# A two-layer hybrid kernel: result places taken in the tile's own unit, moments and first loads issued earlier, three Newton steps, first keys on VectorE

## The chip, the cores and the metric

The kernel runs on one core of one Trainium2 chip. The metric is the device time of one execution in microseconds; the number for a kernel is the median of its timed runs. For the kernel before, three runs gave 991.65, 992.59 and 993.67 us. One further execution was recorded by the hardware profiler.

A core has five engines that work side by side, each on its own instructions in their order: PE (TensorE: matrix products and transposes; its weight loads are listed apart, as PEld), DVE (VectorE), ACT (ScalarE), POOL (GpSimd) and SP (SyncE, which here issues DMA transfers). PE writes to PSUM, from where DVE and ACT take the results into SBUF. An engine waits where an operand is missing or a buffer is still being read.

## The reference

Everything is float32. `x` has the shape [16, 256, 128]: 4096 tokens of 128 channels. Four blocks follow one another, each added to its input:

```python
x = x + attn_a(layernorm(x))     # 16 heads of 8, within blocks of 64 tokens of a sequence
x = x + ffn(layernorm(x))        # router over 8 experts, the best 2 per token
x = x + attn_b(layernorm(x))     # over the first axis (16), for each of 256 positions
x = x + ffn(layernorm(x))        # the same experts and weights again

# ffn
logits = flat_x @ Wr
top_vals, top_idx = top_k(logits, 2);  rw = softmax(top_vals)
g, u = flat_x @ Wg[e], flat_x @ Wu[e]            # [128 -> 512] for an expert e
h = silu(g) * u
out = sum over the two e of rw[e] * (h @ Wd[e]) / sqrt(12)
```

The attention A part has query, key and value biases; attention B first multiplies by `w_tor`, has a toroidal bias on its scores and an output projection. Layer norms have no scale or shift: `(x - mean) / sqrt(var + 1e-5)`.

## The kernel before

**Tokens.** The stream x stays in SBUF as four quarters `xq[q]`, each of 8 groups of 128 rows. A half of a quarter is four groups, 512 rows.

**Stages.** The outer loop runs over two layers, and in each over eight halves `hq` (quarter and half). Layer 0 runs `attention_a` of a half (24 steps), layer 1 `attention_b` (20 steps). After the second half of a quarter comes its `router`: layer norm F, logits, best two, ranks within each expert and, from the second quarter on, the tables of tiles. GpSimd puts each token's normalised row twice into `sorted_in` in DRAM, sorted by expert, with an indirect DMA (L787: one for 128 rows). `experts(layer)` takes the sorted rows as tiles: 256 rows in the first two lists, 128 rows in the last list, whose tiles are known only after the last router. `fetch` (L955, L972) loads a tile's rows `xin` and the three weight matrices `w` of its expert (768 KB) on SP's queue. `turned` makes the tile's transposed rows (`xt` on PE L993, `xT` by ACT L995). Then come the products `g` and `u` (L1055), tanh on ACT (`th` L1066), `th` and `h` on DVE (L1067, L1069), the products down into `acc` (L1006), scaling to `yo` on ACT (L1017), and indirect DMAs by GpSimd to `results` (L1021). The place of each result row stands as one more column of `xin`; the DVE operation `to` (L990) takes it and combines it with the place for padded rows.

The rows of `results` come back with `back` loads (L1102, on SP) and are added to `xq` on DVE (L1117). For layer 1, `begin_b(q)` does this for a quarter, normalises it (`normal_b`) and prepares queries and keys. The numbering `back_0_7` means layer 0, seventh half.

**Order.** `weave(main, *sides)` advances a main generator and hands out the steps of side generators evenly between two of its steps: a side is `(generator, steps, first, last)`. In attention A the sides are the router of the quarter before, `prepare_a` of the next half (layer norm, keys, queries), the `moments` of the half after next, and units of the experts. A scheduler then sets each engine's order from the instructions' priorities and its own cost model, so an engine's order is not exactly that of the program. Each engine executes that fixed order.

**Moments and deviation.** `moments` makes mean and variance on DVE (`st`, `mv`, `ve`); the reciprocal deviation `rs` is a power on GpSimd (L324), or, for attention B (`here=True`), Newton's iteration on DVE (L296-303), where each instruction needs the one before. `layernorm_t` then forms `shift` on DVE (L338), normalises on ACT (`ln`, L345) and transposes on PE (`lnp`, L357).

**Scores of attention A.** Keys and queries are made from PSUM by `four` on ACT (L391), four instructions of 512 columns each. Score products are `sc_A` (L496, PE), the row maximum `mx_A` (L504, DVE), the difference `ex_A` (L505, DVE, which frees the score's PSUM buffer), the exponential (L509, ACT).

In `turned`, called for the next tile while a tile is in work, the first statements are:

```python
to = p12.tile([P, TT // P], I32, tag="to", name=f"to_{s}_{i}")
nc.vector.tensor_tensor(to[:, 0:n], t[:, 0:n, C + 1], elsewhere, ALU.max)
pt = psum(f"xt_{s}_{i}")
```

and in the loop over `hq`:

```python
if hq + 2 < 2 * NQ:
    sides.append((moments_a(hq // 2 + 1, half), 2, n // 2, n))
```

Of the kernel before, what the change touches and what calls it, by code (L numbers as in the profile page):

```python
# [11 lines left out]
I32 = mybir.dt.int32  # L12
# [7 lines left out]
P = 128  # L20
# [94 lines left out]
def hybrid_kernel(  # L115
# [22 lines left out]
    p1 = ctx.enter_context(tc.tile_pool(name="p1", bufs=1))  # L138
    p2 = ctx.enter_context(tc.tile_pool(name="p2", bufs=2))
    p4 = ctx.enter_context(tc.tile_pool(name="p4", bufs=4))  # L140
    p12 = ctx.enter_context(tc.tile_pool(name="p12", bufs=12))
    p3 = ctx.enter_context(tc.tile_pool(name="p3", bufs=3))
    p_in = ctx.enter_context(tc.tile_pool(name="p_in", bufs=2 + AHEAD))
    dram = ctx.enter_context(tc.tile_pool(name="dram", bufs=1, space=bass.MemoryType.DRAM))
# [149 lines left out]
    def rsqrt(out, v, name):  # L294
        seed = p1.tile([P, NG], I32, tag="seed", name=f"seed_{name}")
        work = p1.tile([P, NG], F32, tag="newton", name=f"newton_{name}")  # L296
        nc.vector.tensor_scalar(seed, v.bitcast(I32), 1, None, ALU.logical_shift_right)
        nc.vector.tensor_scalar(seed, seed, -1, 0x5F3759DF, ALU.mult, ALU.add)
        y = seed.bitcast(F32)
        for _ in range(4):  # L300
            nc.vector.scalar_tensor_tensor(work, y, -0.5, y, ALU.mult, ALU.mult)
            nc.vector.tensor_tensor(work, work, v, ALU.mult)
            nc.vector.scalar_tensor_tensor(out, work, 1.5, y, ALU.add, ALU.mult)
            y = out
# [24 lines left out]
    def layernorm_t(q, halves, name, put, keep=None):  # L329
        mv, rstd = stat.pop(name)  # L330
        shift = p2.tile([P, NG], F32, tag="shift", name=f"shift_{name}")
        ln = {}
        for half in halves:
            some = slice(4 * half, 4 * half + 4)
            if keep is None:
                ln[half] = p2.tile([P, 4, C], F32, tag="ln", name=f"ln_{name}_{half}")
            behind_now(
                nc.vector.scalar_tensor_tensor(  # L338
                    shift[:, some], mv[:, some, 0], -1.0, rstd[:, some], ALU.mult, ALU.mult
                )  # L340
            )
            for i in range(4):
                g = 4 * half + i
                behind_act(
                    nc.scalar.activation(  # L345
                        ln[half][:, i, :] if keep is None else keep(g), xq[q][:, g, :],
                        AF.Identity, bias=shift[:, g : g + 1], scale=rstd[:, g : g + 1],
                    )
                )
                if i == 1:  # L350
                    yield
            yield
        for half in halves:
            pt = psum(f"lnp_{name}_{half}")
            for i in range(4):
                g = 4 * half + i
                nc.tensor.transpose(  # L357
                    pt[:, i * P : (i + 1) * P],
                    ln[half][:, i, :] if keep is None else keep(g), ident,
                )  # L360
            put(half, pt)
            yield
# [25 lines left out]
    def four(put, product, scales, biases):  # L388
        for j in range(4):
            behind_act(  # L390
                nc.scalar.activation(  # L391
                    *put(j, product), AF.Identity, bias=biases[:, j : j + 1],
                    scale=scales[:, j : j + 1],
                )
            )
            if j % 2:
                yield

    def product(src, w, name):
        p = ps_gu.tile([P, CH], F32, tag="gu", name=name)  # L400
# [64 lines left out]
    def moments_a(q, half):  # L465
        return moments(q, [half], f"A{q}_{half}", "A")

    def prepare_a(q, half):
        n = f"A{q}_{half}"
        lnT = p2.tile([P, CH // BS, 2, BS], F32, tag="src", name=f"lnT_{n}")  # L470
        qT = p2.tile([P, CH // BS, 4, BS], F32, tag="qT", name=f"q_{n}")
        kx = p2.tile([P, 4, CH], F32, tag="kx", name=f"k_{n}")

        def put(_, pt):
            nc.scalar.copy(*spread(lnT, pt, 2))

        yield from layernorm_t(q, [half], n, put)
        yield from keys(kx, lnT[:, :, 0], wk_sb, B_K, n)
        ready[q, half] = lnT, qT, kx
        yield from queries(qT, lnT[:, :, 0], wq_sb, B_Q, n)  # L480

    def attention_a(q, half):
# [57 lines left out]
    def normal_b(q):  # L540
        lnT = p1.tile([P, BS, S], F32, tag="lnT", name=f"lnB_{q}")

        def put(half, pt):
            nc.scalar.copy(  # L544
                lnT.rearrange("c t s -> c s t")[:, 8 * half : 8 * half + 8, :],
                pt.rearrange("c (s t) -> c s t", t=BS),
            )

        yield from moments(q, range(2), f"B{q}", "B", here=True)
        yield from layernorm_t(q, range(2), f"B{q}", put)  # L550
        ready[q] = lnT.rearrange("c t s -> c (t s)")

# [392 lines left out]
    def experts(layer):  # L945
# [37 lines left out]
                follow(product.ins, stepped)  # L983
            stepped[0] = product.ins

        def turned(li, i, t, elsewhere):
            s = f"{layer}_{li}"
            n = SIZES[li] // P
            to = p12.tile([P, TT // P], I32, tag="to", name=f"to_{s}_{i}")
            nc.vector.tensor_tensor(to[:, 0:n], t[:, 0:n, C + 1], elsewhere, ALU.max)  # L990
            pt = psum(f"xt_{s}_{i}")
            for b in range(n):
                nc.tensor.transpose(pt[:, b * P : (b + 1) * P], t[:, b, 0:C], ident)  # L993
            xT = p2.tile([P, TT], F32, tag="xT", name=f"xT_{s}_{i}")
            nc.scalar.copy(xT[:, 0 : n * P], pt[:, 0 : n * P])  # L995
            return xT, to

# [37 lines left out]
        for at, (li, i) in enumerate(todo):  # L1037
# [3 lines left out]
            if at == 0:  # L1041
                fetched += [fetch(*todo[0]), fetch(*todo[1])]
                begun = 2
                xT, to = turned(*todo[0], fetched[0][0], fetched[0][2])
            t, w, _ = fetched.pop(0)
            acc = ps_acc.tile([P, 512], F32, tag="acc", name=f"acc_{s}_{i}")
            for part in range(NHC // n):
                m = f"{s}_{i}_{part}"
                hcs = range(n * part, n * part + n)

                def product(k, name):
                    p = ps_gu.tile([P, CH], F32, tag="gu", name=f"{name}_{m}")
                    for j, hc in enumerate(hcs):
                        step(
                            nc.tensor.matmul(  # L1055
                                p[:, j * size : (j + 1) * size],
                                lhsT=w[:, k, hc * P : (hc + 1) * P], rhs=xT[:, 0:size],
                                start=True, stop=True,
                            )
                        )  # L1060
                    return p

                pg = product(0, "g")
                pu = product(1, "u")
                th = p2.tile([P, CH], F32, tag="th", name=f"th_{m}")
                turn_of[0] = nc.scalar.activation(th, pg, AF.Tanh, scale=0.5).ins  # L1066
                nc.vector.scalar_tensor_tensor(th, th, 1.0, pg, ALU.add, ALU.mult)  # L1067
                h = p2.tile([P, CH], F32, tag="h", name=f"h_{m}")
                beat[0] = nc.vector.tensor_tensor(h, th, pu, ALU.mult).ins  # L1069

                wanted = at + 2 if size == TT else min(begun + 1, at + AHEAD)
                while begun < len(todo) and part == 0 and begun <= wanted:
                    fetched.append(fetch(*todo[begun]))
                    begun += 1
                if part == 0 and at + 1 < len(todo):
                    following = turned(*todo[at + 1], fetched[0][0], fetched[0][2])
                if pending is not None:
                    down(*pending)
                pending = (li, i, t, w, to, acc, hcs, h)
                yield  # L1080
            xT, to = following
        down(*pending)
        yield

# [98 lines left out]
        yield from normal_b(q)  # L1183
        yield from prepare_b(q, 0)

    BEGIN_A, BEGIN_B = 3 + 4, 5 + 10 + 5
    ALONE = 8

    FIRST = BEGIN[0] + ALONE
# [5 lines left out]
    for layer in range(2):  # L1195
# [10 lines left out]
        for hq in range(2 * NQ):  # L1206
# [5 lines left out]
            if layer == 0:  # L1212
# [4 lines left out]
                    first = n // 6 if hq == 0 else 0  # L1217
                    sides.append((prepare_a((hq + 1) // 2, 1 - half), BEGIN_A, first, 2 * n // 3))
                if hq + 2 < 2 * NQ:
                    sides.append((moments_a(hq // 2 + 1, half), 2, n // 2, n))  # L1220
                wanted, goal = 0, OWN.get(hq, 0)
            else:
                main = attention_b(q, half)
# [2 lines left out]
                elif q < NQ - 2:  # L1226
                    sides.append((begin_b(q + 1), BEGIN_B, 0, 4 * n // 5))
                wanted, goal = (0, GOAL[hq]) if q < NQ - 1 else (1, OWN[hq])
            goal = max(goal, unit[wanted])
            sides.append((units(wanted, goal), goal - unit[wanted], 0, n))  # L1230
            weave(main, *sides)
            if half == 0:
                continue
            run(routing)
            if layer == 1:
                finish_b(q)
                if q == NQ - 2:
                    weave(begin_b(q + 1), (units(1, ALONE), ALONE, 0, BEGIN_B))
            routing = router(layer, q)
        weave(routing, (units(layer, EARLY), EARLY - unit[layer], 0, ROUTER))  # L1240
        run(units(layer, BEGIN[0]))
# [46 lines left out]
```

## Time and profile before

| | |
|---|---|
| median of the timed runs | 992.59 us (991.65 to 993.67) |
| the profiled execution | 941.87 us |
| its span on the core | 939.9 us |
| its mean granted TensorE clock | 0.941 of full speed |
| PE waits at 357.0 and 802.1 us, `u` behind DVE `th` | 5.62 and 5.17 us |
| PE wait at 490.1 us, `lnp_B` behind ACT `ln_B` | 6.61 us |
| PE wait at 643.5 us, `xt` behind the load of `xin` | 6.58 us |
| DVE `th` L1067 (128x512), 142 times | mean 683 ns |
| DVE `va` L443 (128x256 from PSUM) | 0.42 us |
| ACT `xT` L995 (128x256 from PSUM) | 0.37 us |
| ACT keys and queries L391 (128x512 from PSUM) | 0.79 us |

The profiled execution was shorter than the timed ones by 50.7 us. The page does not tell why; all times inside the profile add up to the profiled execution's.

A row of groups or of the timeline names the engine, the line and the operation as output <- inputs. In square brackets, or after the second bar, stands how long the engine had been idle before and which operation's end released it. "Busy in slices" is the busy share in tenths, of 40 equal parts of the span; PEclk is the TensorE clock granted in each, 9 for 90% or more. Records of the granted clock further give stretches at half clock to a microsecond.

### The profile page before, as it was taken

How to read it: one execution, taken by the hardware profiler on the slowest of the kernel's cores; microseconds unless marked ns; L12 is line 12 of the kernel's file. 1: busy time of each engine (PE TensorE's matmuls, PEld its weight loads, DVE VectorE, ACT ScalarE, POOL GpSimd, SP SyncE). 2: the span in 40 equal slices, each digit the busy share in tenths (PEclk: the TensorE clock that was granted, in tenths of full speed). 3: DMA queues.
4: the chain of work that ended last, by engine and by line, in shares of the span. 5: the costliest groups of instructions: out<-in, count | busy, mean ns of one | idle time of the engine just before them, and what ended most of it. 6: DMA issues, size and time to landing. Idle time of an engine off the chain costs nothing.

```text
span 939.9 us, 20600 instructions
## 1 busy us (share of the span) xinstructions
PE 822.3 (87%) x7582; PEld 709.2 (75%) x7582; DVE 552.7 (59%) x1653; ACT 449.2 (48%) x921; POOL 341.6 (36%) x381
## 2 busy tenths in 40 slices
PE   4999799888999997997976979995889999799983
PEld 2777587767889886997764757894668888799983
DVE  2556554564766773456592673683567687355563
ACT  4667367266445332443645635732664533244431
POOL 2113262262256474332101162262314747433321
PEclk9999988799999998999996987998989999899997
DMA  7800010016223626998410023216410452799993
GB/s 165 259 26 1 13 35 2 15 33 237 90 81 109 222 91 217 329 330 322 164 47 1 5 76 88 81 42 227 170 44 27 144 202 89 245 332 331 341 394 109
DMA packets 67011, 134.80 MB, mean 143 GB/s; under 512 B 9088, under 2 KB 46720, under 8 KB 66912
## 3 DMA queue, kind: packets, MB, share of 16 engines
q1 hardware_dynamic: 56400, 114.70, 36.5%
q0 software_dynamic: 8640, 17.97, 5.5%
q8 instruction: 60, 0.98, 0.4%
q10 hardware_dynamic: 1872, 0.83, 0.4%
q14 instruction: 39, 0.32, 0.1%
HBM read 112.33 MB, written 27.43 MB: 149 GB/s over the span
## 4 chain that ended last, share of the span: by engine, by line
PE 41%; DVE 8%; ACT 5%; DMA 4%; issue 2%; POOL 1%; SPq 0%; DVEq 0%; POOLq 0%; ACTq 0%
PE u L1055 9%; PE acc L1006 9%; PE g L1055 9%; PE v_B L437 3%; PE sc_B L600 3%; PE o_B L637 2%; DMA xin<-sorted_in 1%; PE t_B L624 1%; DMA w<-w_all 1%; PE xt_B L559 1%; ACT ln_B L345 1%; DVE th L1067 1%; PE k_B L401 1%; PE xt L993 1%; ACT lnB L544 1%
## 5 line engine op out<-in xcount | busy, mean ns | idle before, releaser
L1021 POOL DMA_INDIRECT results<-yo,to x142 | 137.3, 967 | 248.0 <-ACT yo L1017 178.4
L1067 DVE SCALAR_TENSOR_TENSOR th<-th,g 128x512 f32<-128x512 f32 x142 | 97.0, 683 | 135.4 <-ACT th L1066 134.8
L1055 PE MATMUL u<-xT,w 128*128 128x128 f32 (+1 forms) x864 | 156.7, 316 | 16.3 <-DVE th L1067 16.3
L1055 PE MATMUL g<-xT,w 128*128 128x128 f32 (+1 forms) x864 | 156.5, 316 | 6.4 <-DMA w<-w_all 3.9
L1006 PE MATMUL acc<-w,h 128*128 128x128 f32 x1136 | 155.6, 279 | 1.4 <-DVE h L1069 0.9
L787 POOL DMA_INDIRECT sorted_in<-rows,pos_i_F x128 | 132.1, 1032 | 64.3 <-issue 37.3
L1006 PEld LDWEIGHTS acc<-w,h 128*128 128x128 f32 x1136 | 144.5, 195 | 5.8 <-ACT yo L1017 1.6
L1055 PEld LDWEIGHTS u<-xT,w 128*128 128x128 f32 x864 | 126.5, 196 | 25.8 <-DVE th L1067 18.2
L1066 ACT ACTIVATE th<-g 128x512 f32<-128x512 f32 x142 | 85.0, 598 | 114.9 <-PE g L1055 111.6
L1055 PEld LDWEIGHTS g<-xT,w 128*128 128x128 f32 x864 | 121.8, 195 | 15.8 <-ACT xT L995 6.7
L1069 DVE TENSOR_TENSOR h<-th,u 128x512 f32<-128x512 f32 x142 | 97.1, 683 | 8.8 <-PE u L1055 0.7
L496 PE MATMUL sc_A<-k_A,q_A 128*128 128x256 f32 x256 | 80.6, 434 | 17.9 <-DVE ex_A L505 13.3
L1017 ACT ACTIVATE yo<-acc,xin 128x128 f32<-128x128 f32 x142 | 48.6, 366 | 65.3 <-PE acc L1006 62.8
L526 PEld LDWEIGHTS o_A<-va,eT_A 128*64 128x64 f32 x1024 | 62.2, 142 | 16.6 <-issue 6.9
L995 ACT COPY xT<-xt 128x128 f32<-128x128 f32 (+1 forms) x108 | 32.2, 298 | 80.6 <-PE xt L993 74.5
L496 PEld LDWEIGHTS sc_A<-k_A,q_A 128*128 128x128 f32 x256 | 47.3, 211 | 28.8 <-issue 8.9
L526 PE MATMUL o_A<-va,eT_A 128*64 128x18 f32 x1024 | 67.0, 216 | 0.8 <-ACT eT_A L519 0.7
L504 DVE TENSOR_REDUCE mx_A<-sc_A 128x8 f32<-128x512 f32 x64 | 43.5, 679 | 30.3 <-PE sc_A L496 30.2
L519 ACT COPY eT_A<-t_A 128x512 f32<-128x512 f32 x64 | 36.2, 587 | 44.7 <-PE t_A L515 44.3
L536 POOL TENSOR_TENSOR xq<-xq,att_A 128x128 f32<-128x128 f32 x32 | 14.6, 456 | 116.1 <-DVE att_A L456 89.6
L509 ACT ACTIVATE ex_A<-ex_A 128x512 f32<-128x512 f32 x64 | 39.9, 635 | 31.0 <-DVE ex_A L505 30.8
L505 DVE TENSOR_TENSOR ex_A<-sc_A,mx_A 128x512 f32<-128x512 f32 x64 | 42.8, 680 | 2.0 <-PE t_A L515 1.1
(178 smaller groups left out, 1236.9 us busy)
## 6 DMA issues: line engine op xcount, KB each, us to landing
w<-w_all SPq DMA_DIRECT2D x108, 768.0 KB
back<-results SPq DMA_DIRECT2D x14, 512.0 KB, 4.8
xin<-sorted_in SPq DMA_DIRECT2D x74, 66.0 KB, 3.9
xin<-sorted_in SPq DMA_DIRECT2D x34, 132.0 KB, 3.0
results<-yo,to POOLq DMA_INDIRECT x142, 3.8
w_all<-in_wg SPq DMA_DIRECT2D x1, 2048.0 KB, 15.3
w_all<-in_wu SPq DMA_DIRECT2D x1, 2048.0 KB
w_all<-in_wd SPq DMA_DIRECT2D x4, 512.0 KB
```

Source lines behind the costliest of these rows:

```text
L496: nc.tensor.matmul(sc[:, v * 4 * BS : (v + 1) * 4 * BS], lhsT=qT[:, blk, 2 * v : 2 * v + 2, :].rearrange("p r k -> p (r k)"), rhs=kx[:, :, ...
L504: nc.vector.tensor_reduce(mx[:, 0:8], sc3, AX.X, ALU.max)
L505: beat[0] = nc.vector.tensor_tensor(ex[:, b], sc3, mx[:, 0:8].unsqueeze(2).to_broadcast([P, 8, BS]), ALU.subtract,).ins
L526: nc.tensor.matmul(po[b * BS : (b + 1) * BS, i * 18 : (i + 1) * 18], lhsT=eT[:, b, 2 * v + i % 2, u * BS : (u + 1) * BS], rhs=vt[:, b, 2 * ...
L787: put_row = nc.gpsimd.indirect_dma_start(out=sorted_in[layer], out_offset=bass.IndirectOffsetOnAxis(ap=pos_i[:, k, g : g + 1], axis=0), in ...
L1006: nc.tensor.matmul(acc[:, b * C : (b + 1) * C], lhsT=h[:, j * size + b * P : j * size + (b + 1) * P], rhs=w[:, 2, hc * C : (hc + 1) * C], ...
L1017: nc.scalar.activation(y[:, b, :], acc[:, b * C : (b + 1) * C], AF.Identity, scale=t[:, b, C : C + 1],)
L1021: put_row = nc.gpsimd.indirect_dma_start(out=results[layer], out_offset=bass.IndirectOffsetOnAxis(ap=to[:, b : b + 1], axis=0), in_=y[:, b ...
L1055: nc.tensor.matmul(p[:, j * size : (j + 1) * size], lhsT=w[:, k, hc * P : (hc + 1) * P], rhs=xT[:, 0:size], start=True, stop=True,)
L1066: turn_of[0] = nc.scalar.activation(th, pg, AF.Tanh, scale=0.5).ins
L1067: nc.vector.scalar_tensor_tensor(th, th, 1.0, pg, ALU.add, ALU.mult)
L1069: beat[0] = nc.vector.tensor_tensor(h, th, pu, ALU.mult).ins
```

## The change

Six edits:

- `to` leaves `turned` and becomes `places`, called in the tile's own unit, after `h` of its first part. The pool of 12 buffers goes; `to` now has 4. Instructions are the same.
- Newton's iteration has three steps instead of four.
- `layernorm_t` yields once more between the ACT normalisations and the transposes where it treats two halves (attention B), and `normal_b` once between moments and normalisation. `BEGIN_B`, the number of steps of `begin_b`, goes from 20 to 22.
- Moments for attention A are spread from a quarter to the middle of the main loop instead of from its middle to its end.
- The experts' generator yields after its first two fetches. In layer 0 it is started ahead of the seventh half (`hq == 6`), whose units then begin after a sixth of the loop; in layer 1 ahead of `finish_b` of the third quarter, and the units beside the last `begin_b` begin after a quarter of it.
- The first half's keys and queries come from `keys_and_queries`: both products first, then in two halves of 256 columns the keys on VectorE and the queries on ScalarE.

```diff
-        for _ in range(4):
+        for _ in range(3):
             nc.vector.scalar_tensor_tensor(work, y, -0.5, y, ALU.mult, ALU.mult)
...
+        if len(halves) > 1 and keep is None:
+            yield
         for half in halves:
             pt = psum(f"lnp_{name}_{half}")
...
+    def keys_and_queries(kx, qT, src):
+        pk, pq = product(src, wk_sb, "k_first"), product(src, wq_sb, "q_first")
+        for half in range(2):
+            cols = slice(half * CH // 2, (half + 1) * CH // 2)
+            some = slice(4 * half, 4 * half + 4)
+            for j in range(4):
+                nc.vector.tensor_scalar(
+                    kx[:, j, cols], pk[:, cols], k_sb[:, K_HM + j : K_HM + j + 1],
+                    k_bias[B_K][:, j : j + 1], ALU.mult, ALU.add,
+                )
+                nc.scalar.activation(
+                    qT[:, some, j, :], pq[:, cols].rearrange("p (a k) -> p a k", k=BS),
+                    AF.Identity, bias=q_bias[B_Q][:, j : j + 1], scale=q_scale[:, j : j + 1],
+                )
...
         yield from layernorm_t(q, [half], n, put)
+        ready[q, half] = lnT, qT, kx
+        if (q, half) == (0, 0):
+            keys_and_queries(kx, qT, lnT[:, :, 0])
+            return
...
         yield from moments(q, range(2), f"B{q}", "B", here=True)
+        yield
...
-        def turned(li, i, t, elsewhere):
+        def turned(li, i, t):
             s = f"{layer}_{li}"
             n = SIZES[li] // P
-            to = p12.tile([P, TT // P], I32, tag="to", name=f"to_{s}_{i}")
-            nc.vector.tensor_tensor(to[:, 0:n], t[:, 0:n, C + 1], elsewhere, ALU.max)
             pt = psum(f"xt_{s}_{i}")
...
+        def places(li, i, t, elsewhere):
+            n = SIZES[li] // P
+            to = p4.tile([P, TT // P], I32, tag="to", name=f"to_{layer}_{li}_{i}")
+            nc.vector.tensor_tensor(to[:, 0:n], t[:, 0:n, C + 1], elsewhere, ALU.max)
+            return to
...
                 fetched += [fetch(*todo[0]), fetch(*todo[1])]
                 begun = 2
-                xT, to = turned(*todo[0], fetched[0][0], fetched[0][2])
-            t, w, _ = fetched.pop(0)
+                yield
+                xT = turned(*todo[0], fetched[0][0])
+            t, w, elsewhere = fetched.pop(0)
...
                 beat[0] = nc.vector.tensor_tensor(h, th, pu, ALU.mult).ins
+                if part == 0:
+                    to = places(li, i, t, elsewhere)
...
-    BEGIN_A, BEGIN_B = 3 + 4, 5 + 10 + 5
+    BEGIN_A, BEGIN_B = 3 + 4, 5 + 12 + 5
...
-                    sides.append((moments_a(hq // 2 + 1, half), 2, n // 2, n))
+                    sides.append((moments_a(hq // 2 + 1, half), 2, n // 4, n // 2))
...
+            first = 0
+            if layer == 0 and hq == min(OWN):
+                next(tiles[0])
+                first = n // 6
             goal = max(goal, unit[wanted])
-            sides.append((units(wanted, goal), goal - unit[wanted], 0, n))
+            sides.append((units(wanted, goal), goal - unit[wanted], first, n))
...
             if layer == 1:
+                if q == NQ - 2:
+                    next(tiles[1])
                 finish_b(q)
                 if q == NQ - 2:
-                    weave(begin_b(q + 1), (units(1, ALONE), ALONE, 0, BEGIN_B))
+                    weave(begin_b(q + 1), (units(1, ALONE), ALONE, BEGIN_B // 4, BEGIN_B))
```

## The prediction

> **What bounds the kernel now.** I read the page's first two blocks first, for the engine that sets the end.
>
> ```profile
> PE 822.3 (87%) x7582; PEld 709.2 (75%) x7582; DVE 552.7 (59%) x1653; ACT 449.2 (48%) x921; POOL 341.6 (36%) x381
> PE   4999799888999997997976979995889999799983
> PEclk9999988799999998999996987998989999899997
> ```
>
> TensorE is busy 87% of 939.9 us and no other engine passes 59%; the chain that ended last is PE for 41% too. So only three things shorten the span: less PE work (the change has none: the matmuls are the same), shorter PE gaps, and fewer spells of half clock, the 8s and 7s of PEclk. Going through PE and weight loads together I find 87 us of idle in some forty gaps, and in the clock records fifteen half-clock spells of 3.4 to 13.7 us, together 112 us. An operation is worth what it takes from one of these gaps or spells, and nothing elsewhere. The waits, ordered by engine and releaser (sum, count, longest), say which gaps the change can reach:
>
> ```profile
> DVE to L990 <- DMA xin<-sorted_in: 35.3, 16, 7.9
> PE sc_A L496 <- DVE ex_A L505: 13.3, 11, 4.0
> DVE shift_A L338 <- POOL rs_A L324: 12.1, 6, 4.9
> PE lnp_A L357 <- ACT ln_A L345: 8.9, 1, 8.9
> ```
>
> **1. Moments of attention A sooner** (quarter instead of half of the main loop, to be ended at its middle). The timeline at 112-118 us shows what late moments cost (start, busy, engine, operation, idle before and its releaser):
>
> ```profile
> 114.69 0.96 POOL L787 DMA_INDIRECT sorted_in<-rows,pos_i_F  x1 [0.30 <-issue]
> 115.67 1.04 POOL L324 TENSOR_TENSOR rs_A<-ve_A,minus_half 128x4 f32<-128x4 f32 x1
> 116.75 0.16 DVE L338 SCALAR_TENSOR_TENSOR shift_A<-mv_A,rs_A 128x4 f32<-128x4 f32 x1 [4.93 <-POOL rs_A L324]
> ...
> 117.58 2.08 PE L496 MATMUL sc_A<-k_A,q_A 128*128 128x256 f32 x4 [3.13 <-DVE ex_A L505]
> ```
>
> POOL works in order: rs_A, the power that makes the next quarter's reciprocal deviation, stands behind four puts of sorted rows, 1.27 us apart. VectorE waits 4.93 us for it at shift_A; ex_A, behind shift_A, frees the score buffer, so PE stops 3.13 us. In the new order rs_A stands ahead of the copy of the rows and of all puts of that router: this wait goes. Nothing replaces it: ex_A's operands are ready, and the puts, 1.0 us later, have no reader for some 90 us. The same at 187.4: shift_A waits 3.41 us, PE 1.95 us at lnp_A. After both stand half-clock spells: 116.1 for 6.8 us, 191.2 for 3.4 us. In these the PE does half its work, so they cost 3.4 and 1.7 us.
>
> ```profile
> 110.00:120.00 10.00, 6.65 (x55) 5.43 (x56) 4.10 (x15) 3.86 (x8) 7.83 (x9) 0.81 0.13 43
> 180.00:190.00 10.00, 8.02 (x61) 6.67 (x60) 5.14 (x22) 3.45 (x7) 8.10 (x9) 0.78 0.10 34
> ```
>
> (Columns: window, its length, busy PE, PE loads, DVE, ACT, POOL, then the granted clock: 0.81 and 0.78.)
>
> Here a rule speaks against my sum. The Trainium skill, "TensorE: Matmul & The Clock Gate", section "HAM oscillation", has the clock fall on PE idle of more than about 3.4 us. Neither gap, 3.13 and 1.95 us, is that long, so by the rule the spells come from something else and stay: gain 3.1+1.9 = 5.1 us. By the rows, spells follow stretches whose busy share is only 51-57% (112.7-119) or 52% (187.8-191): gain 5.1+3.4+1.7 = 10.2 us. The rows are this kernel's, so I take 10.2. The rule has this much for it: windows 69-73% busy near 100 us had no spell, so gap and spell aren't one to one.
>
> Of 209.7-213.8 (4.0 us idle, then a 3.4-us spell) I take half: 2.0 + 0.8. There VectorE has the router's moments and tables too, and the new order sets the first expert tile's products behind the score products sc_A of the third and fourth group of the last half, where it was the third alone. About 9.7 us of VectorE work stands before the fourth against 7.7 us of PE work, so 2 us of idle stay. Two jams of VectorE at 101-105 and 171-175 (1.6 and 2.3 us of PE idle), where moments of the next quarter lie now beside max and exponent of scores: 0.9 each. Against these: moments moved to the first half of the loop lie where the normalisation ahead of the router (F) lies. A half's statistics are 0.9 us of VectorE work and three pairs of halves move: 0 to +3, I take +1.8, as PE is 80-99% busy there with products already issued. The spells at 157.1 (13.7) and 177.6 (6.8), after windows 66-79% busy, may go or stay, 0 to -10.2; their own gaps aren't touched, I take 0. Sum: -10.2 - 2.8 - 1.8 + 1.8 = **-13.0** (-24 to -6).
>
> **2. Places of results in the tile's own unit.** The row promises most: 35.3 us of VectorE waits in 16 places. But the largest are these, at the tile lists' ends:
>
> ```profile
> 801.90 0.96 POOL L787 DMA_INDIRECT sorted_in<-rows,pos_i_F  x1 [0.30 <-issue]
> ...
> 804.47 0.33 SPq L955 DMA_DIRECT2D xin<-sorted_in  x1
> ...
> 806.44 0.16 DVE L990 TENSOR_TENSOR to<-xin,behind 128x1 int32<-128x1 f32 x1 [7.45 <-DMA xin<-sorted_in]
> 807.25 2.08 PE L1055 MATMUL u<-xT,w 128*128 128x256 f32 x4 [5.17 <-DVE th L1067]
> ```
>
> The last put leaves POOL at 801.9, xin starts at 804.5, `to` at 806.4, and th, behind it on VectorE, lets PE go after 5.2 us. The twin lies at 357.0-362.7 (5.6 us, `to` waits 7.90). In the order of the changed program `to` of the first two tiles of the last list stands where it stood, ahead of the th of the tile before, in both layers: a scheduler sets the instructions, and the moved line did not move these. So 7.90+1.62+7.45+1.62 = 18.6 of the 35.3 us stay, with both gaps and their two 6.8-us spells. The other 16.7 us lie beside a PE with queued work (of the gaps over 1 us only 760.8, 1.17, and small ones at 313-316, 0.9, meet them). `to` later delays no put: results wait for yo, a full tile later. **-2** (-3 to 0; if the two had moved too, -10 to -17 more).
>
> **3. First keys on VectorE.** At the start ScalarE makes four keys (13.77-16.55) and then four queries; the first score product waits until 17.94, the first max until 20.91. The new keys: 8 of 128x256 from PSUM, near the va row of that shape, 0.42 us, so 3.4 us in two halves of 1.7; queries 8 of half width, near the xT copy, 0.37, or half the spacing of 512-wide ones, 0.35, plus start-up, say 0.45. Query product done at 15.4, half the queries by 17.3, where the fourth was done at 19.2: score products of the first half end 1.8 us sooner. **-1.8** (-2.5 to 0). Nothing else is on VectorE there but the moments of the other half (they'd cost 0.9).
>
> **4. Newton, steps and loads of layer 1.** Three dependent instructions of 0.2 us go from each of four deviations of attention B: 0.6 us each, and in each the PE waits at lnp_B (2.28 at 442, 6.61 at 490, 3.48 at 557), so they count: B0 -0.6, B1 -1.3 (one add of 0.64 us moves behind it as well), B2 -0.8. The extra steps put work between normalisation and transposes, which PE can run instead of waiting. At the beginning of the last part, PE waits 6.58 us for xin and 1.2 for w: issuing the fetches ahead of back_0_7 (two queued loads of 512 KB ahead of them on SP today) brings w 0.8-1.5 us sooner. back_0_7 then lands near 654.6 behind 1.8 MB of tiles; its adds stand behind h at about 657, so I see no stall. -1.5. **Sum -4.2** (-8 to +2).
>
> **Total.** -13.0 - 2.0 - 1.8 - 4.2 = **-21.0 us**, from 941.87 in the profiled execution to 920.9. The median of the timed runs is 992.59, 50.7 us more, which the page doesn't explain; I carry the microseconds over: 992.6 - 21.0 = **971.6**.
>
> **Rivals.**
> - *Large gain:* spells go with the jams, at 157, 177 and in part at 443-505 too: -10.2 more in A, about -5 in B: 992.6 - 36.2 = **956**. For it: 20 us of spells follow windows 66-79% busy. Against: their gaps have releasers the change leaves alone (ln_F, k_A).
> - *Little left:* PE takes up the gained microseconds in the next wait: the router's tables on VectorE (taken, rank) and POOL's puts still end when they did, and both list-end gaps are set by puts. Then only start and Newton stay, -4: **988**. For: POOL 36% busy but back to back from 324 to 362. Against: those puts are tied to PE's tiles, and move up with them.
> - *Slower,* one mechanism: in the last half of attention A the first expert products stand behind the fourth score product. If VectorE, with four groups of F moments ahead of it, comes 3 us later than I say, the gap of 4.0 becomes 7 or more, and the clock falls for 13.7 us, as after 6.61 at 490; with xin of the first tiles displaced and back_0_7 late by 4 us in B, +3 +6.8 +4 and A's gain only -8: +6, **998**. It decides from a gap above 7 us at 210-217. Against: VectorE has 3.1 us of idle at 205-216.
> - That the change doesn't do what it says is, for the two large waits of part 2, my forecast already.
>
> **Numbers.** My forecast 0.55, large gain 0.15, little left 0.14, slower 0.16. The range: own range of the forecast 962-983; reaching to the rivals, **956 to 993**, which leaves out most of "slower" and the low half of "large gain". A difference below 0.2% (2 us) can't be told from none. Faster: 0.55+0.15+0.11 = 0.81; same 0.05; slower 0.14.
>
> **What would show it.** rs_A no longer releases shift_A with over 1 us; no PE gap of 3 us at 114 and no half clock within 110-120 and 188-195; `to` waits for xin only at the lists' ends, about 18 us; gaps of about 5 us at 357 and 802, moved up by what is saved; first max at about 19.1 us; PE idle near 70 us in place of 87. Wrong if clock spells come at new places in attention A, if PE waits at 205-217 for more than 4 us, or if back_0_7 becomes a releaser of PE.

## The result and the profile after

| | median | ratio to before (95% interval) |
|---|---|---|
| before, beside it | 992.88 us (991.65 to 993.67) | |
| changed kernel | 1007.71 us (1003.94 to 1009.86) | 1.0141 (1.0095 to 1.0188) |

The change makes the kernel slower by 14.8 us, where 21 us less were forecast. The changed kernel's page, for the lines shown of before (the last two rows are from the chain that ended last, by engine and by line):

```profile
PE 838.3 (84%) x7582; PEld 714.5 (71%) x7582; DVE 555.7 (55%) x1649; ACT 447.5 (45%) x921; POOL 342.2 (34%) x381
...
PE   5999798889988879979869678967787888799983
...
PEclk9999799999999989998979779987998999999997
...
PE 44%; DVE 16%; DMA 13%; issue 11%; ACT 8%; POOL 4%; another core or an unknown queue 3%; SPq 0%; POOLq 0%; DVEq 0%; ACTq 0%
DMA results<-yo,to 10%; PE acc L1032 6%; PE g L1082 6%; PE u L1082 6%; PE o_A L546 6%; PE sc_A L516 5%; POOL results L1047 3%; PE t_A L535 2%; PE o_B L658 2%; PE sc_B L621 2%; DVE th L1094 2%; PE v_B L454 2%; PE v_A L446 1%; DVE ex_A L525 1%
```

A second trace of the kernel before, of the same kind of chip as this one (before_again, in the experiments below), has TensorE busy for 85% of its span, and its chain by engine is this:

```profile
PE 62%; DVE 12%; ACT 8%; issue 6%; another core or an unknown queue 4%; POOL 4%; DMA 3%; SPq 0%; POOLq 0%; DVEq 0%; ACTq 0%
```

So TensorE does the same 7582 products in about the same share of the span. What is new is the chain that ended last: it rests on transfers for 13% in place of 3%, and 10% is `results<-yo,to`. The waits of the changed kernel (total, times, longest) say who waits for it:

```profile
DVE to L1021 <- DMA results<-yo,to: 130.9, 67, 6.4
...
PE u L1082 <- DVE th L1094: 18.8, 16, 3.0
...
DVE to L1021 <- DMA xin<-sorted_in: 13.4, 4, 6.9
...
DVE shift_A L337 <- POOL rs_A L323: 1.2, 1, 1.2
```

In the kernel before, first profile, the first of these rows was this:

```profile
DVE to L990 <- DMA results<-yo,to: 1.6, 1, 1.6
```

(In before_again it is 1.3 us.) So the wait that the moments were to remove is gone (12.1 us to 1.2), and a new one has come: VectorE waits 130.9 us, 67 times, for result rows to land before it may take the next place.

One thing has to be known for the rest: the kernel before took a different time in different sets of runs, a median of 992.9, 996.5 and 998.6 us in three and 937.0 us in the fourth. The last three were taken on three chips; I call the two kinds slow and quick chips. The first profile, 941.9 us, looks like one of a quick chip. Ratios are therefore always to the kernel before on the same chip, and traces are compared only where they are of the same kind.

### The profile page after: what moved, and what is told of

Same layout as the page of the kernel before. It is cut to its first block, busy times and chain, and to the rows that moved or that the text cites. A ratio compares the mean times of both kernels' runs of the same rounds, so it can differ in the third digit from the quotient of the medians.

```text
span 1002.2 us, 20600 instructions
## 1 busy us (share of the span) xinstructions
PE 838.3 (84%) x7582; PEld 714.5 (71%) x7582; DVE 555.7 (55%) x1649; ACT 447.5 (45%) x921; POOL 342.2 (34%) x381
## 4 chain that ended last, share of the span: by engine, by line
PE 44%; DVE 16%; DMA 13%; issue 11%; ACT 8%; POOL 4%; another core or an unknown queue 3%; SPq 0%; POOLq 0%; DVEq 0%; ACTq 0%
DMA results<-yo,to 10%; PE acc L1032 6%; PE g L1082 6%; PE u L1082 6%; PE o_A L546 6%; PE sc_A L516 5%; POOL results L1047 3%; PE t_A L535 2%; PE o_B L658 2%; PE sc_B L621 2%; DVE th L1094 2%; PE v_B L454 2%; PE v_A L446 1%; DVE ex_A L525 1%
## 5 line engine op out<-in xcount | busy, mean ns | idle before, releaser
L1047 POOL DMA_INDIRECT results<-yo,to x142 | 142.6, 1004 | 267.1 <-ACT yo L1043 201.4
L1082 PE MATMUL u<-xT,w 128*128 128x128 f32 (+1 forms) x864 | 160.0, 319 | 21.2 <-DVE th L1094 18.8
L1032 PE MATMUL acc<-w,h 128*128 128x128 f32 x1136 | 159.8, 283 | 11.5 <-issue 3.7
L1082 PE MATMUL g<-xT,w 128*128 128x128 f32 (+1 forms) x864 | 159.1, 320 | 7.6 <-DMA w<-w_all 5.1
L808 POOL DMA_INDIRECT sorted_in<-rows,pos_i_F x128 | 127.3, 995 | 101.3 <-issue 43.9
L1032 PEld LDWEIGHTS acc<-w,h 128*128 128x128 f32 x1136 | 147.0, 198 | 19.3 <-issue 9.0
L1082 PEld LDWEIGHTS u<-xT,w 128*128 128x128 f32 x864 | 126.7, 197 | 35.6 <-DVE th L1094 24.1
L1082 PEld LDWEIGHTS g<-xT,w 128*128 128x128 f32 x864 | 124.2, 198 | 17.4 <-issue 8.3
L516 PE MATMUL sc_A<-k_A,q_A 128*128 128x256 f32 x256 | 73.9, 407 | 10.5 <-DVE ex_A L525 6.0
L1021 DVE TENSOR_TENSOR to<-xin,behind 128x1 int32<-128x1 f32 x74 | 11.8, 160 | 107.0 <-DMA results<-yo,to 94.6
L516 PEld LDWEIGHTS sc_A<-k_A,q_A 128*128 128x128 f32 x256 | 45.2, 201 | 20.6 <-issue 6.1
```

The lines of the kernel that those rows point to most:

```text
L516: nc.tensor.matmul(sc[:, v * 4 * BS : (v + 1) * 4 * BS], lhsT=qT[:, blk, 2 * v : 2 * v + 2, :].rearrange("p r k -> p (r k)"), rhs=kx[:, :, ...
L808: put_row = nc.gpsimd.indirect_dma_start(out=sorted_in[layer], out_offset=bass.IndirectOffsetOnAxis(ap=pos_i[:, k, g : g + 1], axis=0), in ...
L1032: nc.tensor.matmul(acc[:, b * C : (b + 1) * C], lhsT=h[:, j * size + b * P : j * size + (b + 1) * P], rhs=w[:, 2, hc * C : (hc + 1) * C], ...
L1047: put_row = nc.gpsimd.indirect_dma_start(out=results[layer], out_offset=bass.IndirectOffsetOnAxis(ap=to[:, b : b + 1], axis=0), in_=y[:, b ...
L1082: nc.tensor.matmul(p[:, j * size : (j + 1) * size], lhsT=w[:, k, hc * P : (hc + 1) * P], rhs=xT[:, 0:size], start=True, stop=True,)
```

## The experiments

**Theory W**, formed from the new row: `to` has 4 buffers now in place of 12. A buffer is free only when the put that reads it has landed, so `to` of a tile waits for the puts of the tile four before, and everything behind `to` on VectorE (th, h, vb) waits too. **Theory S**: the extra steps and earlier starts disorder attention B. **Theory U**: moving `to` costs by itself, through the order that the scheduler makes.

The first set, all on one chip, has the kernel before unchanged and three mixtures.

> The kernel before, unchanged, to see its profile beside its timed runs (the first profile, 941.9 us, was 51 us under the median). If that profile was an execution of another kind, this one lies near 992, its added time spread over the attention B and expert stages, with the same half-clock pattern as the changed kernel's; ratio 1.000 within 0.002. If the profiled execution is always shorter than the timed ones, the profile lies near 942 again.

> The changed kernel, with the tile pool of the places `to` back at 12 buffers in place of 4. Theory W (with 4 buffers each place waits on VectorE until the result puts of the tile four before have landed, and th and h stand behind it): the loss goes and the other parts' gain of some 8 us shows: 975 to 990 us, ratio to before 0.985 to 0.997. Theory S (the steps and earlier starts put the attention B stage out of order): stays at 1003 to 1010. Theory U (the move of the place itself, whatever the buffers): also stays above 1000.

```diff
+    p12 = ctx.enter_context(tc.tile_pool(name="p12", bufs=12))
...
-            to = p4.tile([P, TT // P], I32, tag="to", name=f"to_{layer}_{li}_{i}")
+            to = p12.tile([P, TT // P], I32, tag="to", name=f"to_{layer}_{li}_{i}")
```

> The kernel before with edit 1 alone: places taken in the tile's own unit, 4 buffers. Theory W: slower than before by 15 to 25 us, 1007 to 1018 us. Theory S: 990 to 994, as before. Theory U: as W, slower by 15 to 25 us.

 (its edit is the two hunks of `turned` and `places` in the change above, put into the kernel before)

> The changed kernel with edit 1 undone: places taken one tile ahead, 12 buffers; the other five edits stay. Theory W and U: 975 to 990 us. Theory S: 1003 to 1010 us.

 (its edit is the same hunks taken back)

| run | median us | ratio to before on that chip |
|---|---|---|
| before_again | 996.1 | 1.0008 (0.9972 to 1.0045) |
| a_to12 | 970.6 | 0.9752 (0.9678 to 0.9827) |
| b_to4 | 1035.4 | 1.0433 (1.0333 to 1.0532) |
| a_old_to | 971.9 | 0.9737 (0.9659 to 0.9816) |

The kernel before, profiled again, took 995.3 us in that execution, like its timed runs: the 941.9 us of its first profile come from elsewhere (last section). Both kernels with 12 buffers came out 3 to 4 us below the range of W. Eight more buffers of a few bytes per partition turn the loss into a gain. S falls: with all steps and starts in place the kernel is fast. Edit 1 alone costs 4.3%, more than W's 15 to 25 us. W and U are not yet parted, since b_to4 both moves the place and takes buffers away.

How one such wait reaches TensorE can be seen where two traces of slow chips, changed kernel and a_to12, do the same work. First the changed kernel's timeline, in attention B:

```profile
719.43 0.96 POOL L1047 DMA_INDIRECT results<-yo,to  x1 [0.30 <-issue]
...
721.10 0.61 ACT L1093 ACTIVATE th<-g 128x512 f32<-128x512 f32 x1
...
724.69 0.16 DVE L1021 TENSOR_TENSOR to<-xin,no_pads 128x2 int32<-128x2 f32 x1 [5.54 <-DMA results<-yo,to]
724.77 0.68 DVE L1094 SCALAR_TENSOR_TENSOR th<-th,g 128x512 f32<-128x512 f32 x1
725.37 0.68 DVE L460 TENSOR_TENSOR vb<-v_B,k_sb 128x512 f32<-128x512 f32 x1
...
726.10 1.13 PE L580 MATMUL xt_B<-lnB,wt_sb 128*128 128x512 f32 x2 [1.85 <-DVE vb L460]
```

And a_to12 at the same tile:

```profile
690.73 0.96 POOL L1048 DMA_INDIRECT results<-yo,to  x1 [0.30 <-issue]
...
691.62 0.16 DVE L1022 TENSOR_TENSOR to<-xin,no_pads 128x2 int32<-128x2 f32 x1 [1.20 <-DMA xin<-sorted_in]
...
693.01 0.69 DVE L1095 SCALAR_TENSOR_TENSOR th<-th,g 128x512 f32<-128x512 f32 x1 [1.23 <-ACT th L1094]
693.62 0.69 DVE L461 TENSOR_TENSOR vb<-v_B,k_sb 128x512 f32<-128x512 f32 x1
...
695.36 1.02 PE L581 MATMUL xt_B<-lnB,wt_sb 128*128 128x512 f32 x2
```

In the changed kernel the last put of the tile four before was issued at 719.43; `to` may run only at 724.69, 5.3 us later. th, whose tanh began at 721.10, and vb stand behind it, and TensorE is idle for 1.85 us for vb. In a_to12 `to` runs 0.9 us after the corresponding put, th waits only for its tanh, and TensorE does not stop.

The second set, on another chip, asks for the number of buffers and for the worth of the other edits.

> The changed kernel with 6 buffers for the places in place of 4 (12 gave 970.6 us, 4 gave 1007.7 us). Theory W (a place waits for the landing of the puts of so many tiles before; the waits with 4 are 2.0 us on average and 6.4 us at most, and two more tiles of 2.8 us each give 5.6 us): nearly all of the loss is gone, 970 to 978 us, and VectorE's waits for results are under 20 us in place of 131. Rival, that the number of buffers acts through the order that the scheduler plans and not through a wait: somewhere between, 985 to 1000 us, or as with 4.

 (the pool above with 6)

> The changed kernel with 12 buffers and the moments of attention A back in the second half of the loop. Theory A (moments sooner take 13 us out of attention A, as the prediction had it): 980 to 986 us, shift_A again waits over 10 us for rs_A. Rival (the other edits make the gain, the puts' stretch costs the same either way): 969 to 974 us.

```diff
-(moments_a(hq // 2 + 1, half), 2, n // 4, n // 2)
+(moments_a(hq // 2 + 1, half), 2, n // 2, n)
```

> The changed kernel with 12 buffers and the earlier start of the first loads undone in both layers. By the prediction's 1.5 us for layer 1, and nothing for layer 0: 970 to 974 us. Rival, that the first loads ahead of the back loads are a larger part of the gain of 6 us seen in attention B: 976 to 980 us.

```diff
-                yield
                 xT = turned(*todo[0], fetched[0][0])
...
-                next(tiles[0])
-                first = n // 6
...
-                    next(tiles[1])
...
-ALONE, BEGIN_B // 4, BEGIN_B)
+ALONE, 0, BEGIN_B)
```

> The changed kernel with 12 buffers, four Newton steps and no extra steps beside attention B's normalisation. By the prediction (0.6 to 1.3 us per deviation, four of them): 973 to 975 us. Rival, that the extra steps let PE pass the wait at lnp_B (3.5 to 5 us in each of three places): 980 to 985 us.

```diff
-        for _ in range(3):
+        for _ in range(4):
...
-        if len(halves) > 1 and keep is None:
-            yield
...
-        yield
         yield from layernorm_t(q, range(2), f"B{q}", put)
...
-5 + 12 + 5
+5 + 10 + 5
```

| run | median us | ratio to before on that chip (998.6 us) |
|---|---|---|
| a_to6 | 992.9 | 0.9937 (0.9902 to 0.9972) |
| a12_mom_late | 985.4 | 0.9805 (0.9716 to 0.9894) |
| a12_starts_off | 975.4 | 0.9794 (0.9730 to 0.9858) |
| a12_b_off | 980.4 | 0.9831 (0.9775 to 0.9887) |

The expectation for 6 buffers missed: nearly half of the loss stays, not a tenth. It took the life of a place from the last list alone (below). The time lies where its rival, the scheduler's order, had it; the third set comes back to this. The other three lie above the ratio of the changed kernel with 12 buffers on the other chips, 0.975 to 0.977 (a_to12 above, a_to12_more below), by 0.3 to 0.8%, with intervals that overlap: by these runs none of the parts can be sized well, or told from none with certainty. Of two of them the traces show what the edit does to its wait. (For the earlier loads no such row stands out.) The kernel with late moments has back the row of before:

```profile
DVE shift_A L338 <- POOL rs_A L324: 12.4, 6, 4.9
```

And the kernel without the edits to attention B's normalisation, first row, waits longer for it at `lnp_B` than a_to12, second fence:

```profile
PE lnp_B L357 <- ACT ln_B L345: 15.0, 3, 6.6
```

```profile
PE lnp_B L359 <- ACT ln_B L345: 8.5, 3, 4.8
```

The third set, on a quick chip, parts W from U.

> The kernel before with the place taken in the tile's own unit, as in edit 1, but with the 12 buffers kept. With 4 buffers this gave 1035.4 us. Theory W (the buffers alone make the loss): 992 to 998 us, ratio to before 0.996 to 1.002. Theory U (the move reorders the engines, and this costs too): 1010 us or more.

 (b_to4 with the 12 buffers kept)

> The kernel before with nothing changed but the pool of the places: 4 buffers in place of 12, the place still taken one tile ahead. Theory W, by lifetimes: a place lives from its making until its last put has landed, in the last list 6.4 us to the put and 4.9 us from there, 11.3 us in all with the move, and one tile of 2.8 us longer without it; 4 tiles last 11.2 us. So it must lose at least as much as with the move: 1030 to 1060 us. Theory U: 1000 us or less.

```diff
-    p12 = ctx.enter_context(tc.tile_pool(name="p12", bufs=12))
+    p12 = ctx.enter_context(tc.tile_pool(name="p12", bufs=4))
```

> The changed kernel with 8 buffers for the places. By lifetimes: 8 tiles of 2.8 us last 22 us, beyond the 11.3 us of the last list; what is left are the stretches in which the own put comes 25 to 45 us after the place: 972 to 982 us, between 970.6 (12) and 992.9 (6).

> The changed kernel with 12 buffers once more, on the chip of the three others: 965 to 975 us, ratio to before 0.970 to 0.980.

| run | median us | ratio to before on that chip (937.0 us) |
|---|---|---|
| b_to12 | 938.3 | 1.0013 (0.9995 to 1.0030) |
| b_old4 | 973.9 | 1.0406 (1.0366 to 1.0445) |
| a_to8 | 916.2 | 0.9775 (0.9735 to 0.9816) |
| a_to12_more | 915.6 | 0.9767 (0.9728 to 0.9807) |

(The expectations in us were written for a chip at 993 to 998 us; by ratio, b_old4 was expected at 1.03 to 1.06.) One number changed in the kernel before, 12 to 4, costs 4.1%; moving the place with 12 buffers costs nothing that can be told. U falls.

The order of VectorE's instructions, read from the traces, says why, and what is left of the rival that buffers act through the order. In b_to12 the order is that of the kernel before, all 1653 in the same places: with 12 buffers the scheduler sets `to` where it stood, though the program has it later. With 4 (b_old4) it sets `to` behind one or more further `th` in 55 of the 108 places, and 13 of the other 1545 instructions move. A later `to` has less left to wait for, yet it waits longer. And in a_to6, a_to8 and a_to12 every one of the 108 `to` stands behind the same `th`; between 6 and 12 buffers no more than 6 other instructions of VectorE and none of ScalarE and GpSimd move, but 6 lose 1.7 to 1.9%. So it is the wait that costs. The waits of b_old4:

```profile
DVE to L990 <- DMA results<-yo,to: 122.8, 63, 6.3
...
PE u L1055 <- DVE th L1067: 29.2, 20, 4.7
```

And of b_to12:

```profile
DVE to L999 <- DMA xin<-sorted_in: 33.9, 15, 7.9
...
PE u L1059 <- DVE th L1071: 15.7, 5, 5.6
...
DVE to L999 <- DMA results<-yo,to: 1.5, 1, 1.5
```

These two traces, of the same chip, show what the 122.8 us of waiting cost: b_old4's span is 32.6 us longer (970.8 after 938.2). TensorE and its loads, taken together, are idle 24.1 us more in gaps over 0.3 us (111.4 after 87.3), and the half-clock spells last 11.9 us longer (131.5 after 119.6), some 6 us of work. The rest of the waiting lies beside a TensorE with work in its queue.

**How many buffers are needed** can be counted, and in the trace of the kernel before alone. A place lives from `to` until its tile's last put has landed, which the page of before has at a median of 3.8 us after the issue. At the start of each of the 108 `to`, I count the places that still live, itself among them:

| live places | 1 to 4 | 5 | 6 | 7 |
|---|---|---|---|---|
| times, before | 26 | 32 | 36 | 14 |

By this count 82 of 108 places would have to wait with 4 buffers, 14 with 6 and none with 8. The runs follow it: ratios of 1.014, 0.994 and 0.978 with 4, 6 and 8, and 0.977 with 12. The traces have 67 waits for results with 4 (63 in b_old4), one of 1.7 us with 8, and with 6 these, 28.9 us where under 20 were expected:

```profile
DVE to L1022 <- DMA results<-yo,to: 28.9, 15, 6.1
```

In the regular stretches of the last lists a place of the kernel before waits 8.9 to 12.5 us for its own put, and with the landing lives 12.7 to 16.3 us; tiles come every 2.79 us, so it needs five to six buffers. Among the large tiles the put comes 13 to 88 us after the place, 40 us in the middle, since units of experts are spread thin there; this is where my expectation for 6 went wrong.

**The best version** is the changed kernel with 8 or 12 buffers, faster than both kernels: 0.9775 (0.9735 to 0.9816) and 0.9767 (0.9728 to 0.9807) of the time before.

## Why the prediction was wrong

**The step that failed is part 2's price of the moved place**: "`to` later delays no put: results wait for yo, a full tile later. -2 (-3 to 0...)". It looked from the place forwards, to who reads it, and not backwards, to whose buffer it takes. The change gives the place 4 buffers in place of 12; no term stands for that. Measured, 4 buffers cost 4.1% on the kernel before (b_old4) and 1.0141/0.9767, or 3.8%, on the changed one: some 38 us of 993. The "slower" rival put the slowing elsewhere, in the last half of attention A, and so did not foresee it either. The move that was priced at -2 is worth 0 (b_to12, where VectorE's order is that of before).

The same part held that 18.6 of the 35.3 us that `to` waits for xin would stay, and 16.7 go. In the changed kernel 13.4 us stay, in 4 places, but only because `to` stands later there and waits 130.9 us for results. With 12 buffers 33.9 us stay (b_to12): the scheduler keeps the place, and so its wait, where it was. That the two large gaps at the lists' ends stay was right; in a_to12_more they are 4.67 and 5.20 us after 5.62 and 5.17.

**The rest of the sum held in total.** Without the buffers' loss the forecast was -21.0 us and 971.6 us; a_to12 took 970.6 us, 25.9 under before on its chip, and a_to12_more is 21.4 us under before. That the total came so near is in part luck: some terms were too large and some too small, and traces of equal orders differ by several us. Point by point, a_to12_more's trace against b_to12's, of the same chip (b_to12 has before's order):

- *Moments sooner, -13.0*: at the thirteenth `th`, behind attention A, it is 15.8 us ahead (275.9 after 291.7), of which 2.5 stem from the start: -13.3. By a_to8's trace it is -10.4 (278.8). The run with late moments alone, on another chip, gets there at 301.9, where a12_b_off and a12_starts_off have 288.4 and 291.7. So a size of 10 to 13 us at the end of attention A is shown; in the medians over the whole kernel it is only partly seen (a ratio of 0.9805 after 0.975 to 0.977). The waits at shift_A are down to one of 1.2 us, and the gaps of TensorE of 3.13 and 1.95 us are gone. Of the gap of 4.0 us, of which half was to stay, 1.44 is left.
- *The clock*: I took the spells behind these gaps, 6.8 and 3.4 us, to go with them, against the rule of the Trainium skill ("TensorE: Matmul & The Clock Gate", "HAM oscillation") that gaps over some 3.4 us bring them. In sum this was right, spell by spell it was not. Half clock in attention A adds up to 34 to 61 us in the six traces with late moments (34.1 in before and in b_to12) and to 17 to 27 us in seven of the eight with sooner ones (20.4 in a_to12_more; the eighth, a_to6, has 44.5). On one chip, late moments alone have 44.3 (a12_mom_late), sooner ones 17.0 and 27.2 (a12_b_off, a12_starts_off). From 34.1 to 20.4 are 6.8 us of work, near the 5.9 that I took. But a_to12_more has two spells of 10.2 us, at 103.8 and 161.8, so half clock within 110-120 came after all and new places did too, which the prediction had among its signs of being wrong; and b_to12 has no spell behind its gap of 1.87 us at 185.3. The windows of a_to12_more show that a spell can come without a gap (columns as in the prediction):

```profile
100.00:110.00 10.00, 9.08 (x87) 8.39 (x86) 4.32 (x14) 3.08 (x6) 5.10 (x6) 0.69 0.09 30
110.00:120.00 10.00, 9.80 (x62) 7.50 (x62) 4.04 (x9) 5.30 (x8) 7.67 (x10) 0.80 0.14 47
172.00:182.00 10.00, 9.77 (x91) 7.63 (x90) 6.82 (x32) 6.68 (x12) 8.07 (x9) 1.00 0.17 56
```

  The clock is 0.69 in a stretch where TensorE is 91% busy: the slow clock itself lengthens the products and so may make up part of this share. No gap over 0.9 us lies in the 80 us ahead of the spell at 103.8. How long gaps must be can't be read from such rows, nor which gap brings which spell; that the sooner moments go with less half clock can be read from the sums.
- *First keys on VectorE, -1.8*: first maximum at 18.2 after 20.7 us, -2.5. Right in kind, 0.7 too small.
- *Newton, steps and loads, -4.2*: from the thirteenth `th` to the last the lead grows by 8.6 us (15.8 to 24.4), and by 13.1 in a_to8's trace. Too small by half or more: the extra steps, to which I gave no number, let TensorE pass part of the wait at lnp_B. The gap of 6.61 us is 3.54, that of 3.48 is gone. The other terms here were too large: the first wait at lnp_B, 2.28 us and 2.38 for `th` just ahead of it, is now one of 4.77, and of the 1.5 us of the loads 0.45 came (5.79 and 1.73 us of waiting after 6.66 and 1.31). The run without the steps and with four Newton iterations, ratio 0.9831, lies nearer to the rival of that expectation, but its interval reaches down to the forecast.
- *TensorE's idle* was to fall from 87 to near 70 us: 73.0 (both in gaps over 0.3 us, of which before has 68, not some forty).

## What to carry to other kernels

A buffer count is part of a data movement: count, at each write of a tile, how many earlier ones still have a reader, a DMA's landing included, in the trace that you have. Where the count exceeds the buffers, the writer waits on its engine, and everything behind it in that engine's order waits with it, however small the write. Moving the write in the program does not shorten the life if the scheduler sets it early again, as it did in b_to12; the order stands in the trace.

## What the runs showed that was not expected

**The same kernel differs by 6% from chip to chip.** It takes 937.0 us on one chip and 996.5 and 998.6 us on two others. Each chip was timed in one set only, so it isn't shown that the chip, and not the hour, makes the difference. The added time shows in a trace of a slow chip as pauses for which no releaser is found. The rows of before_again at the values of attention B, 64 products in bursts:

```profile
563.69 1.61 PE L437 MATMUL v_B<-wi_sb,xt_B 128*32 128x128 f32 x49
...
565.49 0.45 PE L437 MATMUL v_B<-wi_sb,xt_B 128*32 128x128 f32 x5 [0.19 <-issue]
...
566.22 0.44 PE L437 MATMUL v_B<-wi_sb,xt_B 128*32 128x128 f32 x6 [0.28 <-issue]
...
566.95 0.43 PE L437 MATMUL v_B<-wi_sb,xt_B 128*32 128x128 f32 x4 [0.29 <-issue]
...
567.74 0.66 PE L624 MATMUL t_B<-k_sb,ex_B 128*128 128x128 f32 x4 [0.36 <-DVE vb L443]
...
572.97 0.58 ACT L630 COPY eT_B<-t_B 128x512 f32<-128x512 f32 x1 [8.66 <-remote]
...
573.61 0.47 PE L993 MATMUL xt<-k_sb,xin 128*128 128x128 f32 x1 [5.21 <-ACT eT_B L630]
```

The same place in the first profile of before:

```profile
546.86 1.95 PE L437 MATMUL v_B<-wi_sb,xt_B 128*32 128x128 f32 x64
```

1.95 us there, 3.7 us here (563.69 to 567.38), and then 5.2 us of idle until ScalarE's eT_B, which has been idle for 8.66 us itself; "remote" means that the profile names no releaser on this core. Product by product, before_again ends 53.6 us behind the first profile, and most of it is lost in stretches in which GpSimd puts sorted rows. What a slow chip does then was not tried; it stays open. The change was timed on a slow chip, but the loss by 4 buffers in the kernel before is much the same on both kinds: 4.3% (b_to4, slow) and 4.1% (b_old4, quick), two kernels that differ only in where the program has `to`.
